# Layer 1's column products as eight 64x64 products in four array tiles, fed from a second copy of the own rows

## The chip, the cores and the metric

The kernel runs on one core of a Trainium2 chip. The metric is device time in microseconds. Three timed runs of the kernel before gave 908.75, 901.74 and 906.34 us, median 906.34 us. The profiled execution is a run of its own: 909.48 us, of which 907.7 us lie between the first and the last instruction. TensorE's granted clock over that execution was 0.957 of full speed.

## The reference, cut to what matters

A graph attention layer with four heads, then a second attention layer with one head, a residual and two layer norms, over 8 batches of 2048 nodes with 64 channels:

```python
h = einsum('bnc,hdc->bhnd', x, Wh)                       # 4 heads
scores = where(mask, einsum('...nd,...md->...nm', h, h), NEG)
out_h = einsum('...nm,...md->...nd', softmax(scores), h) + bh
z = leaky_relu(cat, 0.2);  h2 = einsum('bnk,dk->bnd', z, Wo)
# the same attention on h2 (one head), leaky_relu, layernorm
out = layernorm(x + that)
```

The mask is the adjacency matrix with its diagonal set. The graph given is sparse away from its first nodes, and the fast path of the kernel uses that. Because scores of layer 1 are `x_n Wh^T Wh x_m`, the kernel forms the 64x64 matrix `Wh^T Wh` of each head once (called `gram`) and multiplies only the rows of the attending nodes with it.

## The kernel before, in words

**Tiling.** 56 hub nodes (`HUB`) are treated apart, against all nodes, in a first stage. The other 1992 nodes form 166 sets of 12 (`SET`). For each set, the neighbours of its nodes are found from the adjacency matrix as a list of at most 128 nodes. Two sets make a group `g` (83 groups, `NG`). A tile holds two batches on its 128 partitions, 64 channels each (called the two halves below), and four such pairs `q` side by side.

**Layer 1's loop** is one Python loop over `i` from -4 to NG+2; one pass is called a step here. Its order is written out by hand, so each engine runs its instructions in the order in which the step emits them. Each step works on several groups at different depths. TensorE's order within a step is:

- L836 `scores`: 64x64 products of the gathered, turned rows `xTg` with the columns `y`.
- L532 `project`: 64x64 products of 96 columns with `whT`, in four array tiles (row half `s` by column half `j`).
- L861 `values`: 128x64 products of the weights `e` with gathered rows `g`.
- L895 `second_maps` (128x64), L905 `second_rows` (a 96-wide transpose), then L821 `columns`, then L513 `turn` (four 128x128 transposes of gathered rows), L878 `turn_values` (transposes of `osb`), L513 again, and the next step's L836.

**Columns.** `own_rows` (L815, on POOL, each second step) copies the rows of four sets out of `xT` into the tile `xo`, 128 partitions by 192 columns. `columns(g)` multiplies `xo` with `gram` for two heads: two products of 128x128 by 192 columns. `gram` is a 128x128 matrix for each head with the 64x64 matrix on both diagonal blocks and zeros elsewhere, so both halves are done at once. The result is copied by ACT (L827 `keep_columns`) into `y`, which `scores` uses later. The POOL copy emitted in step `i` serves the products of steps `i+2` and `i+3`.

**The other engines in a step.** POOL: two indirect gathers (L807, five groups ahead), each second step L815, in the first nine steps an adjacency piece (L689, and L696 after each second piece), from step 30 on each second step `add_beta` (L943), then L901, which copies the tile `own` out. DVE: L841 (mask the scores), L868 and L869 (divide the values, writing `osb`), L524, L900 (writes `own`; the tile has two buffers, so it waits for POOL's L901 of two steps before), L909 (writes `rowt`), and jobs of the neighbour search. ACT: L519, L1146 (two copies that free the banks of L513), L848, L827, L885.

**SP's queue** issues the transfers, in the order of the program: adjacency pieces (L684, one in each of steps 0 to 8, 480 KB each, read by POOL's L689 of the same step into one of three buffers), `table2`'s rows (L912, two in each step, waiting for DVE's L909), and from step 30 on in each even step eight loads of x (L939 `load_own`, 24 KB each), which POOL's L943 reads in the odd step after; L944 stores L943's result.

A second stage (layer 2) follows from about 602 us, which the change doesn't touch.

Of the kernel before, what the change touches and what calls it, by code (L numbers as in the profile page):

```python
# [30 lines left out]
F32 = mybir.dt.float32  # L31
# [328 lines left out]
def fast_kernel(ctx: ExitStack, tc: tile.TileContext, x, adj, Wh, bh, Wo, bo, gamma, beta, out, flag):  # L360


    nc = tc.nc
    B, N, C = x.shape
    H, D, _ = Wh.shape
    P = 128
    NB = N // P
    Q = B // 2
    HP = H // 2
# [4 lines left out]
    NS = (N - HUB) // SET  # L374
    NG = NS // 2
    M = SET * H
    GM = 2 * Q * SET
# [13 lines left out]
    work = stage.enter_context(tc.tile_pool(name="work", bufs=2))  # L391
# [7 lines left out]
    def half(k):  # L399
        return slice(k * 64, (k + 1) * 64)  # L400
# [14 lines left out]
    share = [const.tile([P, n], F32, name=f"share{k}") for k, n in enumerate([HALFN, HALFN, HALFN, 512, 512, 2 * 456])]  # L415
    wnat = share[3][:, :H * C].rearrange("p (h c) -> p h c", h=H)
    whT = early.tile([P, H * D], F32, name="whT")
    gram = early.tile([P, H, P], F32, name="gram")
# [93 lines left out]
        for q in range(Q):  # L512
            nc.tensor.transpose(tp[:, q * P:(q + 1) * P], rows[:, q, 1:1 + P], ident)  # L513

    def leaky(cat, n, name):

        z = work.tile([P, HP, 2, n], F32, tag="z", name=name, bufs=3)
        for hp in range(HP):
            nc.scalar.activation(z[:, hp], cat[:, :, hp * n:(hp + 1) * n], AF.Identity, bias=bhp[:, hp:hp + 1], scale=1.0)  # L519
        return z  # L520

    def leak(z):
        f = z.rearrange("p q s n -> p (q s n)")
        nc.vector.scalar_tensor_tensor(f, f, SLOPE, f, OP.mult, OP.max)  # L524

    def project(ot, cat, n):

        for hp in range(HP):
            for s in range(2):
                for j in range(2):  # L530
                    h = 2 * hp + j
                    nc.tensor.matmul(cat[half(j), s, hp * n:(hp + 1) * n], whT[half(s), h * D:(h + 1) * D],  # L532
                                     ot[half(s), h, :], start=True, stop=True)
# [97 lines left out]
    def hub_later(t, new):  # L631

        n = 2 * HUB
        osb = hub_osb[t]

        def turn_back():
            pt = bank[0]
            for v in range(2):
                for k in range(2):
                    nc.tensor.transpose(pt[:, (2 * v + k) * P:(2 * v + k + 1) * P], osb[:, v, k, :], ident)  # L640
            ot = held["oth", t] = work.tile([P, H, n], F32, tag="ot", name=f"otbh{t}")
            nc.scalar.copy(ot.rearrange("c h (w n) -> c h w n", w=8),  # L642
                           pt.rearrange("c (w n) -> c w n", w=8)[:, :, :HV].rearrange("c w (n h) -> c h w n", h=H))

        def through_heads():
            cat = new(f"cath{t}", "C")
            project(held.pop(("oth", t)), cat, n)
            z = held["zh", t] = leaky(cat, n, f"zh{t}")
            leak(z)

        def to_table():
            z = held.pop(("zh", t))
            ph = new(f"hh{t}", "S")
            for p in range(2):
                for hp in range(HP):

                    v = z[:, hp, p, :].rearrange("d (v k m) -> d k v m", v=2, k=2)
                    nc.tensor.matmul(ph[half(p), 0, :n], woT[:, hp, :], v, start=(hp == 0), stop=(hp == HP - 1))
            nc.vector.tensor_copy(ownh[:, t, :], ph[:, 0, :n])
            nc.tensor.transpose(ph[:n, 1, :P], ownh[:, t, :], ident)  # L660
            r = rowts[t]
            nc.vector.tensor_tensor(r[:n, 1:1 + P], ph[:n, 1, :P], bob[:n].rearrange("n p d -> n (p d)"), OP.add)
            dst = table2[:HUB, :].rearrange("n (q c) -> q n c", q=Q)
            for k in range(2):
                nc.sync.dma_start(out=dst[2 * t + k], in_=r[k * HUB:(k + 1) * HUB])

        return [turn_back, through_heads, to_table]

    hub_osb = {}
# [130 lines left out]
    held = {}  # L800
# [9 lines left out]
    def own_rows(m):  # L810

        w = min(4, NS - 4 * m)
        t = held["x", m] = work.tile([P, 2 * GM], F32, tag="xo", name=f"xo{m}", bufs=2)
        src = xT[:, :, HUB:].rearrange("c q (k s) -> c s q k", s=NS)[:, 4 * m:4 * m + w]
        nc.gpsimd.tensor_copy(t[:, :w * 48].rearrange("c (s q k) -> c s q k", s=w, q=Q), src)  # L815

    def columns(g, cat):

        n = min(4, NS - 4 * (g // 2)) * 48
        for k in range(2):  # L820
            nc.tensor.matmul(cat[:, k, 2 * GM:2 * GM + n], gram[:, g % 2 * 2 + k, :], held["x", g // 2][:, :n], start=True, stop=True)  # L821

    def keep_columns(g, cat):
        n = min(4, NS - 4 * (g // 2)) * 48
        if g % 2 == 0:
            held["y", g // 2] = work.tile([P, 2 * GM, H], F32, tag="yg", name=f"y{g // 2}", bufs=2)
        nc.scalar.copy(held["y", g // 2][:, :n, g % 2 * 2:g % 2 * 2 + 2], cat[:, :, 2 * GM:2 * GM + n].rearrange("p a n -> p n a"))  # L827

    def scores(g, sp):
        xt = held.pop(("T", 1, g)).rearrange("c j (q n) -> c j q n", q=Q)  # L830
# [184 lines left out]
    for g in range(LOOK - 2):  # L1015
        for j in range(2):
            gather(table1, 2 * g + j, 1, rows_tile)
    own_rows(0)
    own_rows(1)
    for t in range(2):  # L1020
        hub_end(t)
# [9 lines left out]
    def one(name, tag):  # L1031
        return psum1.tile([P, 2, 512], F32, tag=tag, name=name)
# [94 lines left out]
    for i in range(-4, NG + 3):  # L1127
# [6 lines left out]
        cat = one(f"cat{i}", "C") if i <= NG else None  # L1134
        if i < NG:
            ph, pr = cat[:, 0, 384:384 + GM], cat[:GM, 1, 384:512]
        else:
            cat = one(f"cat{i}", "S" if i == NG + 1 else "C")
            ph, pr = cat[:, 0, :GM], cat[:GM, 1, :P]
        if 0 <= i - 1 < NG:  # L1140
            project(held.pop(("ot", i - 1)), cat, GM)
            held["z", i - 1] = leaky(cat, GM, f"z{i - 1}")
        if 0 <= i + 2 < NG:
            t = held["T", 1, i + 2] = work.tile([P, 2, 512], F32, tag="xTg", name=f"xTg{i + 2}", bufs=3)
# [11 lines left out]
        if NG - LOOK <= i < NG - 1:  # L1156
            for j in range(2):
                k = 2 * (i - NG + LOOK) + j
                hub_block(k, rows_tile(f"gh{k}"))
        if i + 6 < NG and i % 2 == 0 and i >= -2:  # L1160
            own_rows((i + 6) // 2)
# [25 lines left out]
        if 0 <= i + 4 < NG + NG % 2:  # L1187
            columns(i + 4, cat)
# [7 lines left out]
        if 0 <= i + 4 < NG + NG % 2:  # L1196
            keep_columns(i + 4, cat)
# [226 lines left out]
    k = 9  # L1424
    for u in range(-3, NU + 5):
        if 0 <= u < NU:
            a = u % 2
# [10 lines left out]
        if 0 <= u + 1 < NU:  # L1438
            a = (u + 1) % 2
# [31 lines left out]
def gat_kernel(tc: tile.TileContext, x, adj, Wh, bh, Wo, bo, gamma, beta, out):  # L1471
    nc = tc.nc
    with tc.tile_pool(name="flags", bufs=1, space=bass.MemoryType.DRAM) as pool:
        flag = pool.tile([1, 1], I32, name="flag")
        with tc.manual_schedule():
            fast_kernel(tc, x, adj, Wh, bh, Wo, bo, gamma, beta, out, flag)
        again = nc.values_load(flag, min_val=0, max_val=1)
        with tc.If(again > 0):
            general_kernel(tc, x, adj, Wh, bh, Wo, bo, gamma, beta, out)
# [28 lines left out]
```

## Time and profile before

| what | value |
|---|---|
| three timed runs | 901.74 to 908.75 us, median 906.34 |
| profiled execution, span | 909.48 us, 907.7 us |
| first stage and start of layer 1's loop | 0 to 155.5 us |
| layer 1's steps 0 to 29 | 155.5 to 325.2 us |
| steps 30 to 73 | 325.2 to 553.1 us |
| steps 74 to the end of the loop | 553.1 to about 602 us |
| TensorE's products for the columns (L821) | 320 matmul records of 326 ns each in the loop |
| adjacency pieces (L684) after 155 us | 7 of 34, 170.6 to 206.8 us |
| loads of x (L939) | 168, 324.7 to 536.3 us |

How to read it: a page gives sums over the whole execution; the timeline gives single instructions, with the start, the duration, the engine, the program line, the operation, the tiles (written <- read), the count when several are merged, and in brackets how long the engine had been idle and what ended that. SPq and POOLq are the engines' own instruction queues, where transfers are issued. Products in fp32 show as two records each.

### The profile page before, as it was taken

The numbers are of one execution on the slowest core, as the hardware profiler recorded it, in microseconds if no ns is written. First come the engines' busy times: TensorE is split into PE (matmuls) and PEld (weight loads), VectorE is DVE, ScalarE is ACT, GpSimd is POOL, SyncE is SP. The second block draws the span as 40 slices with busy tenths as digits, with TensorE's granted clock in tenths as the row PEclk, the third lists the DMA queues.
The fourth block names the chain that finished last, engine by engine and source line by source line (L and its number), as shares of the span: only waits on it lengthen the run. The fifth ranks groups of instructions, "written<-read, shape, count | busy, mean of one in ns | idle before, by whom it ended". The sixth has DMA issues, their size and how long they took to land.

```text
span 907.7 us, 42895 instructions
## 1 busy us (share of the span) xinstructions
PE 777.0 (86%) x18437; PEld 660.8 (73%) x18437; DVE 613.0 (68%) x1376; ACT 524.7 (58%) x1128; POOL 540.8 (60%) x780
## 2 busy tenths in 40 slices
PE   4777778899999999999999999989988887878750
PEld 3555456678889998989998988878867776666540
DVE  3247974678988788775566566543677877777594
ACT  1333443555666767667676666735667766667541
POOL 4553241556455456656666665128888888888810
PEclk9899988999999999999999999999999999999975
DMA  8885540354333344444544443339756565555521
GB/s 182 234 238 174 138 117 24 111 134 118 88 82 94 86 117 134 129 125 135 132 125 121 125 125 99 104 111 287 197 151 170 167 166 165 145 151 153 149 68 28
DMA packets 81792, 122.54 MB, mean 135 GB/s; under 512 B 35568, under 2 KB 51852, under 8 KB 81594
## 3 DMA queue, kind: packets, MB, share of 16 engines
q0 software_dynamic: 26784, 65.84, 27.8%
q1 hardware_dynamic: 37702, 49.57, 18.2%
q10 hardware_dynamic: 17108, 4.30, 2.5%
q8 instruction: 148, 2.42, 1.1%
q14 instruction: 50, 0.41, 0.2%
HBM read 123.91 MB, written 18.48 MB: 157 GB/s over the span
## 4 chain that ended last, share of the span: by engine, by line
PE 51%; DVE 16%; POOL 11%; DMA 9%; issue 6%; ACT 4%; SPq 1%; POOLq 0%; ACTq 0%; DVEq 0%
PE o L861 9%; PE s L836 8%; POOL rows L807 8%; PE bank L513 7%; PE cat L821 5%; DMA raw<-in_adj_dram 5%; PE cat L532 3%; PE o L878 3%; DMA rows<-table,index 3%; PE t L513 3%; PE cat L895 3%; PE o L1279 2%; POOL space L1235 2%; PE cat L905 2%; DVE share L746 1%
## 5 line engine op out<-in xcount | busy, mean ns | idle before, releaser
L807 POOL DMA_INDIRECT g<-table,index x166 | 176.4, 1063 | 171.7 <-PE o L861 137.1
L807 POOL DMA_INDIRECT rows<-table,index x166 | 174.8, 1053 | 35.3 <-issue 18.3
L841 DVE TENSOR_TENSOR e<-s,mask 128x768 f32<-128x768 f32 x83 | 79.3, 955 | 79.4 <-PE s L836 75.7
L513 PE MATMUL t<-ident,rows 128*128 128x128 f32 x664 | 97.6, 283 | 35.7 <-DMA rows<-table,index 22.4
L513 PEld LDWEIGHTS t<-ident,rows 128*128 128x128 f32 x664 | 73.8, 143 | 52.7 <-issue 20.6
L519 ACT ACTIVATE z<-cat,bhp 128x192 f32<-128x192 f32 x166 | 60.7, 417 | 78.8 <-PE cat L532 78.7
L1398 ACT COPY xts<-t 128x512 f32<-128x512 f32 x166 | 90.6, 586 | 25.0 <-PE t L513 24.7
L513 PE MATMUL bank<-ident,g 128*128 128x128 f32 x664 | 100.7, 275 | 0.2 <-ACT otbh L642 0.2
L861 PE MATMUL o<-g,e 128*64 128x65 f32 x2656 | 96.5, 225 | 0.6 <-issue 0.6
L836 PE MATMUL s<-y,xTg 64*64 64x48 f32 x5312 | 95.4, 220 | 0.7 <-DVE share L717 0.7
L836 PEld LDWEIGHTS s<-y,xTg 64*64 64x64 f32 x5312 | 85.2, 134 | 14.6 <-issue 14.6
L861 PEld LDWEIGHTS o<-g,e 128*64 128x64 f32 x2656 | 84.7, 137 | 10.6 <-issue 0.7
L1146 ACT COPY xTg<-bank 128x512 f32<-128x512 f32 x166 | 89.1, 596 | 0.8 <-PE bank L513 0.8
L513 PEld LDWEIGHTS bank<-ident,g 128*128 128x128 f32 x664 | 80.3, 142 | 3.0 <-DVE keysi L774 0.6
L848 ACT ACTIVATE e<-e,shifts 128x768 f32<-128x768 f32 x83 | 80.0, 964 | 2.4 <-DVE e L841 2.0
L606 ACT ACTIVATE e<-e,shifts 128x896 f32<-128x896 f32 x32 | 33.3, 1043 | 79.5 <-DVE e L603 46.9
L689 POOL TENSOR_SCALAR a<-raw 120x1024 bf16<-120x1024 int32 (+1 forms) x34 | 38.2, 1128 | 67.7 <-DMA raw<-in_adj_dram 61.7
L827 ACT COPY y<-cat 128x384 f32<-128x384 f32 (+1 forms) x80 | 40.7, 509 | 65.3 <-DVE rowt L909 31.5
L821 PE MATMUL cat<-xo,gram 128*128 128x192 f32 (+1 forms) x320 | 65.0, 326 | 0.0
L868 DVE RECIPROCAL rall<-o 64x8 f32<-64x8 f32 x166 | 34.0, 205 | 43.6 <-PE o L861 42.0
L1279 PE MATMUL o<-rows,share 128*32 128x65 f32 x2656 | 52.7, 234 | 8.6 <-DVE share L1268 8.6
L869 DVE TENSOR_TENSOR osb<-o,rall 128x512 f32<-128x512 f32 x83 | 57.4, 691 | 2.9
(191 smaller groups left out, 1575.4 us busy)
## 6 DMA issues: line engine op xcount, KB each, us to landing
raw<-in_adj_dram SPq DMA_DIRECT2D x32, 480.0 KB
table<-xb SPq DMA_DIRECT2D x22, 256.0 KB
xr_s<-table SPq DMA_DIRECT2D x21, 256.0 KB
table<-x SPq DMA_DIRECT2D x16, 260.0 KB
x<-in_x_dram ACTq DMA_DIRECT2D x32, 128.0 KB
table<-rowt SPq DMA_DIRECT2D x164, 24.4 KB
xb<-in_x_dram SPq DMA_DIRECT2D x164, 24.0 KB
out_dram<-y_s SPq DMA_DIRECT2D x162, 24.0 KB
```

The costliest lines, as they stand in the source:

```text
L513: nc.tensor.transpose(tp[:, q * P:(q + 1) * P], rows[:, q, 1:1 + P], ident)
L519: nc.scalar.activation(z[:, hp], cat[:, :, hp * n:(hp + 1) * n], AF.Identity, bias=bhp[:, hp:hp + 1], scale=1.0)
L807: nc.gpsimd.indirect_dma_start(out=t.rearrange("n q c -> n (q c)"), out_offset=None, in_=table, in_offset=bass.IndirectOffsetOnAxis(ap=ind ...
L821: nc.tensor.matmul(cat[:, k, 2 * GM:2 * GM + n], gram[:, g % 2 * 2 + k, :], held["x", g // 2][:, :n], start=True, stop=True)
L836: nc.tensor.matmul(sp[half(r), p, (q * 2 + j) * M:(q * 2 + j + 1) * M], xt[half(p), j, q, half(r)], y[half(p), (j * Q + q) * M:(j * Q + q ...
L841: nc.vector.tensor_tensor(e[:, :16 * M].rearrange("p (a q n) -> p a q n", a=2, q=Q), sp[:, :, :8 * M].rearrange("p a (q n) -> p a q n", q= ...
L848: nc.scalar.activation(e[:, :16 * M], e[:, :16 * M], AF.Exp, bias=shifts[:, 0:1], scale=1.0)
L861: nc.tensor.matmul(op[half(p), j, o0:o0 + K1], e[:, c0:c0 + 64], rw[j][:, q, sums(p)], start=True, stop=True)
L869: nc.vector.tensor_tensor(osb, v[:, :, :, 1:K1], r.unsqueeze(3).to_broadcast([P, 4, 2, D]), OP.mult)
L1146: nc.scalar.copy(t[:, k, :], bank[k])
L1279: nc.tensor.matmul(op[t * 32:(t + 1) * 32, f, k * W2 + p:k * W2 + p + K1], e[:, 2 * q + p, k, :], rw[:, q, sums(p)], start=(a == 0 and k = ...
L1398: nc.scalar.copy(xts[s // 2 % 4][:, s % 2, :], tp)
```

## The change

`own_rows` issues, after POOL's copy, two transfers on SP's queue that copy each half of `xo`, the part that the other half of the array needs, into a new tile `xs` (128 partitions by 96 columns, two buffers). `columns` then makes each head's product as four 64x64 products of 96 columns: row half `r` of the array with the block of `gram` there, column half `p` of the array for the output. Where `r` equals `p` the moving operand is `xo`, else `xs`. So all four 64x64 tiles of the array take part, and each has half the columns. The copy out of PSUM (`keep_columns`) reads the new layout. To make room, the two hub tiles `zh` move from the ring of `z` into a tile that is free then (`share[5]`), which makes the ring's slots smaller.

```diff
-    def leaky(cat, n, name):
+    def leaky(cat, n, name, z=None):
-        z = work.tile([P, HP, 2, n], F32, tag="z", name=name, bufs=3)
+        if z is None:
+            z = work.tile([P, HP, 2, n], F32, tag="z", name=name, bufs=3)
...
-            z = held["zh", t] = leaky(cat, n, f"zh{t}")
+            z = share[5][:, t * 4 * n:(t + 1) * 4 * n].rearrange("p (a b n) -> p a b n", a=HP, b=2)
+            held["zh", t] = leaky(cat, n, f"zh{t}", z)
...
         nc.gpsimd.tensor_copy(t[:, :w * 48].rearrange("c (s q k) -> c s q k", s=w, q=Q), src)
+        other = held["xs", m] = work.tile([P, GM], F32, tag="xs", name=f"xs{m}", bufs=2)
+        n = w * 24
+        for p in range(2):
+            nc.sync.dma_start(out=other[half(p), :n], in_=t[half(1 - p), p * n:(p + 1) * n])
...
-        n = min(4, NS - 4 * (g // 2)) * 48
+        n = min(4, NS - 4 * (g // 2)) * 24
+        t, other = held["x", g // 2], held["xs", g // 2]
         for k in range(2):
-            nc.tensor.matmul(cat[:, k, 2 * GM:2 * GM + n], gram[:, g % 2 * 2 + k, :], held["x", g // 2][:, :n], start=True, stop=True)
+            h = g % 2 * 2 + k
+            for p in range(2):
+                for r in range(2):
+                    src = t[half(p), r * n:(r + 1) * n] if r == p else other[half(r), :n]
+                    nc.tensor.matmul(cat[half(p), r, 2 * GM + k * n:2 * GM + (k + 1) * n], gram[half(r), h, half(r)], src,
+                                     start=True, stop=True)
...
-        nc.scalar.copy(held["y", g // 2][:, :n, g % 2 * 2:g % 2 * 2 + 2], cat[:, :, 2 * GM:2 * GM + n].rearrange("p a n -> p n a"))
+        nc.scalar.copy(held["y", g // 2][:, :n, g % 2 * 2:g % 2 * 2 + 2].rearrange("p (r n) k -> p r n k", r=2),
+                       cat[:, :, 2 * GM:2 * GM + n].rearrange("p r (k n) -> p r n k", k=2))
```

Lines below the first edit move down: L684 becomes L686, L912 L925, L939 L952, L944 L957, L943 L956, L815 L817, L901 L914, L900 L913; the new transfers stand at L821 and the new products at L832.

The first place is SP's queue in steps 2 to 5 of the loop (`raw` is an adjacency piece, `rowt` a row that goes to the second table). Before:

```order
L684 DMA raw_0_1_1892<-in_adj_dram 120x1x1024
L684 DMA raw_1_0_2017<-in_adj_dram 120x1x1024
L665 DMA table_99<-rowt_112 56x130 x2
L684 DMA raw_1_1_2140<-in_adj_dram 120x1x1024
L684 DMA raw_2_0_2272<-in_adj_dram 120x1x1024
L912 DMA table_99<-rowt_112 4x12x130 x2
L665 DMA table_99<-rowt_113 56x130 x2
L684 DMA raw_2_1_2400<-in_adj_dram 120x1x1024
```

and now:

```order
L821 DMA xs_1919<-xo_1917 64x96 x2
L686 DMA raw_0_1_1928<-in_adj_dram 120x1x1024
L686 DMA raw_1_0_2058<-in_adj_dram 120x1x1024
L667 DMA table_99<-rowt_112 56x130 x2
L821 DMA xs_2180<-xo_2178 64x96 x2
L686 DMA raw_1_1_2190<-in_adj_dram 120x1x1024
L686 DMA raw_2_0_2327<-in_adj_dram 120x1x1024
L925 DMA table_99<-rowt_112 4x12x130 x2
L667 DMA table_99<-rowt_113 56x130 x2
L821 DMA xs_2460<-xo_2458 64x96 x2
L686 DMA raw_2_1_2464<-in_adj_dram 120x1x1024
```

In each even step the two copies into `xs`, the first of which waits for POOL's copy into `xo`, now stand ahead of the adjacency piece of that step.

The second place is the same queue from step 30 on (`xb` is the tile that the eight loads of x fill). Before:

```order
L939 DMA xb_148<-in_x_dram 12x2x256 x8
L912 DMA table_99<-rowt_115 4x12x130 x2
L944 DMA table_150<-xb_148 128x512
L912 DMA table_99<-rowt_112 4x12x130 x2
L939 DMA xb_149<-in_x_dram 12x2x256 x8
```

and now:

```order
L821 DMA xs_5688<-xo_5686 64x96 x2
L952 DMA xb_148<-in_x_dram 12x2x256 x8
L925 DMA table_99<-rowt_115 4x12x130 x2
L957 DMA table_150<-xb_148 128x512
L925 DMA table_99<-rowt_112 4x12x130 x2
L821 DMA xs_5941<-xo_5939 64x96 x2
L952 DMA xb_149<-in_x_dram 12x2x256 x8
```

The eight loads of an even step stood right behind the odd step's row transfers; now the two copies into `xs`, with their wait for POOL, stand between.

The third place is TensorE's queue in one step, from `second_rows` to the next `scores`. Before:

```order
L905 MATMUL cat_3433<-ident,own_3372 96x128
L821 MATMUL cat_3433<-xo_3118,gram 128x192 x2
L513 MATMUL bank_1710<-ident,g_32_3241 128x128 x4
L878 MATMUL o_3449<-ident,osb_3466 128x112 x4
L513 MATMUL bank_1711<-ident,g_33_3245 128x128 x4
L836 MATMUL s_3512<-y_3153,xTg_3445 64x48 x32
```

and now:

```order
L918 MATMUL cat_3179<-ident,own_3119 96x128
L832 MATMUL cat_3179<-xo_2970,gram 64x96
L832 MATMUL cat_3179<-xs_2972,gram 64x96 x2
L832 MATMUL cat_3179<-xo_2970,gram 64x96 x2
L832 MATMUL cat_3179<-xs_2972,gram 64x96 x2
L832 MATMUL cat_3179<-xo_2970,gram 64x96
L513 MATMUL bank_1716<-ident,g_26_2962 128x128 x4
L891 MATMUL o_3195<-ident,osb_3212 128x112 x4
```

Two products on the whole array, between transposes that also use it whole, have become eight on its quarters.

## The prediction

> **What bounds the kernel now.** I read the page first, then one step of layer 1's loop in the timeline, then the timeline of POOL and SP alone, because the change gives those two queues work. The page's busy times and its chain:
>
> ```profile
> PE 777.0 (86%) x18437; PEld 660.8 (73%) x18437; DVE 613.0 (68%) x1376; ACT 524.7 (58%) x1128; POOL 540.8 (60%) x780
> ...
> PE 51%; DVE 16%; POOL 11%; DMA 9%; issue 6%; ACT 4%; SPq 1%; POOLq 0%; ACTq 0%; DVEq 0%
> ```
>
> TensorE holds half of the chain, but that is a mean over stages. The changed work lies in layer 1's loop. One step of it in the timeline, with some rows of PEld (weight loads), DVE and ACT:
>
> ```profile
> 304.75 0.53 PE L532 MATMUL cat<-otb,whT 64*64 64x96 f32 x16
> ...
> 305.21 1.15 PE L861 MATMUL o<-g,e 128*64 128x65 f32 x32
> ...
> 306.62 0.31 PE L905 MATMUL cat<-ident,own 128*96 128x128 f32 x1
> ...
> 306.77 0.82 PE L821 MATMUL cat<-xo,gram 128*128 128x192 f32 x4
> 306.86 0.69 DVE L869 TENSOR_TENSOR osb<-o,rall 128x512 f32<-128x512 f32 x1
> ...
> 307.43 0.60 PE L513 MATMUL bank<-ident,g 128*128 128x128 f32 x4
> ...
> 307.75 0.45 PEld L878 LDWEIGHTS o<-ident,osb 112*128 112x128 f32 x4
> ...
> 307.86 0.55 PE L878 MATMUL o<-ident,osb 112*128 112x112 f32 x4
> ...
> 308.25 0.60 PE L513 MATMUL bank<-ident,g 128*128 128x128 f32 x4
> ...
> 308.78 1.15 PE L836 MATMUL s<-y,xTg 64*64 64x48 f32 x64
> ...
> 308.87 0.54 ACT L885 COPY otb<-o 128x192 f32<-128x192 f32 x2
> ...
> 309.75 0.53 PE L532 MATMUL cat<-otb,whT 64*64 64x96 f32 x16
> ```
>
> No PE row carries a bracket: TensorE waits for nothing, and from L532 to L532 a step takes 309.75 - 304.75 = 5.00 us. In such a step every tenth that TensorE saves is a tenth of time, until another engine's chain is in the way. Not all steps are like this:
>
> ```profile
> L861 PE MATMUL o<-g,e x2656: 218/222/271, 155.5 to 594.6; 128*64 128x65 f32 x190
> ```
>
> Between the starts of L861's 83 groups, 51 of the 82 distances in the timeline lie within 0.1 us of 5.00; the others are longer, with other engines ending them (a few at the end are shorter).
>
> **The products.** From L905 to L513 the step now takes 307.43 - 306.62 = 0.81 us. What replaces L821 has a twin: L532 is also eight 64x64 products of 96 columns in four tiles, and takes 305.21 - 304.75 = 0.46 us up to the next group's start, which has another array shape. Ahead of it stand L905's own 128 columns (four transposes of that size take 307.86 - 307.43 = 0.43 us, so 0.11) and the change of shape into 64x64: from the second L513 to L836 is 0.53 us for the same four transposes, so 0.10 more. Sum 0.11 + 0.10 + 0.46 = 0.67: **0.14 us less a step**. Bounds: 0.24 if the change of shape into the products were free, and a loss of 0.19 if only two tiles overlapped (the body 0.33 longer; the new loop has the row half innermost, L532 the column half). I take 0.14, since L532 is the same shape.
>
> The Trainium skill has a rule against this change: its page TensorEngine Tiling (Array Packing), Key Properties, says that a change of tiling mode drains TensorE. The 0.10 us above agrees with it, and by it the change adds two such drains a step; by its table of theoretical speedups alone an estimate would be nearer 0.33, half of L821's 0.66.
>
> Is there room for 0.14? `osb` is ready at 306.86 + 0.69 = 307.55 and L878's weights are loaded from 307.75: 0.20 of slack, enough. ACT's L885 ends at 309.41, 0.34 ahead of L532. The copy L827 keeps its 384 elements a partition; if its new pattern cost it 0.1, that slack would take it. Moving the hub tiles costs nothing: the same activations write them, and if their tile were not free they would wait in two steps alone.
>
> **The copies.** They move 84 x 24 KB, 2 MB beside 122.5 MB, so bandwidth is no term. The term is SP's queue: the first copy of an even step waits for POOL's L815, and what SP has to issue behind it waits as well. In steps 0 to 8 that is the adjacency piece which POOL's L689 reads in the same step; from step 30 on it is the eight loads that POOL's L943 reads in the next. In both places POOL then waits for a transfer that itself waited for POOL: a ring. Such a ring has a length of its own, whatever TensorE does.
>
> *The ring from step 30 on.* POOL and SP over two steps, the shortest loads on which POOL visibly waited, a pair of row transfers for the cost of issuing, and the columns that would use the copy:
>
> ```profile
> 449.91 1.04 POOL L807 DMA_INDIRECT g<-table,index  x1 [1.12 <-PE o L861]
> 450.30 3.47 SPq L939 DMA_DIRECT2D xb<-in_x_dram  x8
> 451.26 1.02 POOL L807 DMA_INDIRECT g<-table,index  x1 [0.30 <-PE cat L821]
> 452.28 0.53 POOL L815 COPY xo<-xT 128x192 f32<-128x192 f32 x1
> ...
> 457.66 1.27 POOL L943 TENSOR_TENSOR xb<-xb,bet 128x512 f32<-128x512 f32 x1 [0.38 <-DMA xb<-in_x_dram]
> 458.89 0.26 POOL L901 COPY own<-own 128x96 f32<-128x96 f32 x1
> ...
> 460.15 0.82 PE L821 MATMUL cat<-xo,gram 128*128 128x192 f32 x4
> ```
>
> ```profile
> 169.75 0.77 SPq L665 DMA_DIRECT2D table<-rowt  x2
> ...
> 347.89 4.11 SPq L939 DMA_DIRECT2D xb<-in_x_dram  x8
> ...
> 353.97 1.27 POOL L943 TENSOR_TENSOR xb<-xb,bet 128x512 f32<-128x512 f32 x1
> ```
>
> ```profile
> L943 POOL TENSOR_TENSOR xb<-xb,bet x22: 1267/1282/1292, 333.9 to 551.1; 128x512 f32<-128x512 f32 x22
> ```
>
> The ring in its order: an even step's gathers and L815, 449.91 to 452.81, 2.90; to SP and the two copies' issue, 0.05 + 0.77 (for 64 rows of 384 B the nearest is L665, 56 rows of 520 B, twice); from the first of the eight loads to L943, 353.97 - 347.89 = 6.08; L943 and L901, 459.15 - 457.66 = 1.49; to the next even gather about 0.15, as after other L901. Sum **11.4 us for two steps**. Before, the loads stand ahead of the gathers, and 21 distances of L943 take 551.1 - 333.9 = 217.2, or 10.34 each. So the ring falls behind by 1.1 a pair, 23 us in all. A lag of some 4 us costs nothing: the copy would land at about 452.81 + 0.05 + 0.77 + 2.3 = 455.9 (2.3 is from the start of the last of the eight issues, 0.4 before 352.00, to L943 at 353.97), and its products start at 460.15. That leaves **+19**. Bounds: with the other pass in which POOL waited, 457.66 - 450.30 = 7.36, the ring is 12.7 and the term 21 x 2.36 - 4 = +46; with 5.3, the landing of a bigger transfer below, it is 10.65 and the term +2.
>
> *The ring of steps 0 to 8.* POOL's busy time over those steps (the columns of the row are the stretch, its length, then PE, PEld, DVE, ACT and POOL), and single rows:
>
> ```profile
> 156.80:214.70 57.90, 51.12 (x1282) 44.39 (x1281) 41.98 (x111) 33.65 (x78) 36.88 (x49) 1.00 0.47 126
> ```
>
> ```profile
> 170.61 1.70 SPq L684 DMA_DIRECT2D raw<-in_adj_dram  x2
> ...
> 175.90 1.09 POOL L689 TENSOR_SCALAR a<-raw 120x1024 bf16<-120x1024 int32 x1 [1.84 <-DMA raw<-in_adj_dram]
> ...
> 186.91 1.52 SPq L684 DMA_DIRECT2D raw<-in_adj_dram  x1
> ...
> 193.92 1.14 POOL L689 TENSOR_SCALAR a<-raw 120x1024 bf16<-120x1024 int32 x1 [3.56 <-DMA raw<-in_adj_dram]
> ...
> 205.35 0.26 POOL L901 COPY own<-own 128x96 f32<-128x96 f32 x1
> ...
> 210.54 0.26 DVE L900 COPY own<-cat 128x96 f32<-128x96 f32 x1
> ...
> 214.36 0.26 POOL L901 COPY own<-own 128x96 f32<-128x96 f32 x1
> ...
> 223.88 0.27 POOL L901 COPY own<-own 128x96 f32<-128x96 f32 x1 [1.60 <-DVE own L900]
> ```
>
> A piece lands 175.90 - 170.61 = 5.3 to 193.92 - 186.91 = 7.0 us after its issue. Now POOL's 36.9 us have 21 of idle time between them, of which 5.4 is for pieces. With the change each of the five even steps waits 0.8 + 5.3 = 6.1 behind L815: 36.9 + 5 x 6.1 + 2.7 (nine gaps of 0.30 between gathers) = 70.1, so step 8's L901 ends near 227 instead of 214.6, 12 late, and step 6's 6 to 7 late. Who waits: DVE's L900 writes the tile that L901 of two steps before must have left. Step 8's L900 (210.54) has 210.54 - 205.61 = 4.9 of slack, step 10's (ending at 223.88) about 9. So TensorE, which waits for DVE through L909, L827 and L885, loses about 2 in step 8 and 2 in step 10: +4 with 5.3, by the same count +12 with 7.0. I take **+6**, nearer the pair that was issued without delay.
>
> *Sum.* The 0.14 is won only where no ring sets the pace: some 25 steps (12 to 30 and 76 on), -3.5. So -3.5 + 6 + 19 = +21.5. On the profiled execution's 909.5 that makes 931; the median of the runs shown is 3.1 lower, so **928 us**.
>
> **The rivals.** *Hidden copies.* They are issued two steps ahead of their use, SP is idle much of the time, and POOL in the page is only 60% busy; then the products' gain remains: 51 steps x 0.14 = 7, and about 1 from the start of the loop, so 898. For it speaks that the rings are about time to land, which the trace shows only with other neighbours; against it, that in two passes POOL already waits for these very loads with SP a whole row of transfers earlier. The Trainium skill's page DMA: Bandwidth & Descriptors, Rules for kernel authors, advises just this (issue early, wait late, and the fixed cost overlaps); it does not speak of what queues behind a transfer that has to wait for its source.
>
> *Only the early ring binds.* If the loads land in 5.3, the late term is +2 and the gain is won in most steps: -5.5 + 6 + 2 = +2.5, so 909.
>
> *Long landings.* With 7.36 the sum is -3.5 + 6 + 46 = +48.5, so 955.
>
> *Two tiles only.* If the four tiles don't overlap, the change doesn't do what it says: 0.19 longer in the 25 free steps, +5 instead of -3.5, so 936. L532's 0.46 speaks against it.
>
> **How the numbers follow.** Forecast (both rings bind) 0.60, own range 915 to 946; hidden copies 0.13; only the early ring 0.14; long landings 0.06; two tiles 0.07. The range that holds eight in ten is 898 to 948: below it lies half of the hidden case, above it the long landings and the forecast's tail. Faster by over 1% (below 897), which is about what a measurement of this kernel can tell from no change: 0.06. Within 1%: 0.07 from the hidden case, 0.11 from the early ring alone, 0.03 from the forecast's low end, 0.21. Slower by over 1%: 0.73.
>
> **What would show it.** Right: L943's instruction starts 11 to 12 us apart and its idle time is put down to the transfers into `xb`; L689 waits some 5 us in even steps 0 to 8; the products' line in even steps waits for the transfers into `xs`, and DVE's L900 for POOL's L901; in steps 12 to 30 the step is 4.86. Wrong: steps at 4.86 after step 40 (the late ring does not bind), or L905 to L513 at 0.81 or more (the products are no faster).

## The result and the profile after

The changed kernel takes **956.54 us** (median of 4 runs) where the kernel before takes 904.04 us (4 runs): 1.0568 times, 95% interval 1.0513 to 1.0624. On another chip the same pair measured 957.45 against 909.26, 1.0501 (1.0424 to 1.0577). (The ratios and intervals here and below are taken from undisturbed runs alone, and can differ by some thousandths from the quotient of the two medians.) So it is slower by some 50 us, in the forecast's direction and beyond its range of 898 to 948. The profiled execution took 956.55 us, span 954.8.

The page's busy times and its chain:

```profile
PE 796.3 (83%) x19445; PEld 655.6 (69%) x19445; DVE 613.6 (64%) x1376; ACT 525.6 (55%) x1128; POOL 538.9 (56%) x780
...
PE 37%; POOL 18%; DVE 15%; DMA 12%; issue 9%; ACT 4%; SPq 3%; POOLq 1%; ACTq 0%; DVEq 0%
```

TensorE has 1008 more product records, and its share of the chain falls from 51% to 37%; POOL goes from 11% to 18%, transfers from 9% to 12%, SP's queue from 1% to 3%. What grew is, for the most part, what passes through POOL and SP.

**Where the time is.** ACT's exponentials stand once in each of the 83 groups. Their row in the kernel before (count, duration, first and last start), and then after:

```profile
L848 ACT ACTIVATE e<-e,shifts x83: 935/965/968, 153.9 to 589.8; 128x768 f32<-128x768 f32 x83
```

```profile
L861 ACT ACTIVATE e<-e,shifts x83: 935/965/974, 148.9 to 638.8; 128x768 f32<-128x768 f32 x83
```

The loop takes 489.9 us instead of 435.9: **54.0 us more**, all of the loss. (The loop of the kernel before starts 5 us later in its profiled execution, since TensorE's granted clock fell to 0.52 to 0.83 in parts of 132 to 152 us there; in the traces of two kernels below it starts at 147 us.) Single starts of the same rows, read from the timelines:

```
group        0      13      33      40      50      60      70      82
before  153.90  232.41  336.89  372.50  424.86  475.28  528.34  589.81
after   148.93  235.44  341.79  383.90  444.44  506.68  565.87  638.78
shift    -4.97   +3.03   +4.91  +11.40  +19.58  +31.40  +37.52  +48.97
```

So the early steps lose 8.0, groups 13 to 33 lose 1.9, and the rest loses **44.1**.

**The late ring.** POOL over one turn, then SP's transfers in it:

```profile
442.18 1.27 POOL L956 TENSOR_TENSOR xb<-xb,bet 128x512 f32<-128x512 f32 x1 [4.29 <-DMA table<-rowt]
443.41 0.25 POOL L914 COPY own<-own 128x96 f32<-128x96 f32 x1
443.83 1.04 POOL L809 DMA_INDIRECT g<-table,index  x1 [0.17 <-PE o L874]
...
446.13 1.02 POOL L809 DMA_INDIRECT g<-table,index  x1 [1.25 <-PE o L891]
447.15 0.51 POOL L817 COPY xo<-xT 128x192 f32<-128x192 f32 x1
...
454.87 1.26 POOL L956 TENSOR_TENSOR xb<-xb,bet 128x512 f32<-128x512 f32 x1 [4.51 <-DMA table<-rowt]
```

```profile
447.69 1.18 SPq L821 DMA_DIRECT2D xs<-xo  x2
448.91 4.08 SPq L952 DMA_DIRECT2D xb<-in_x_dram  x8
```

The order is the one predicted: POOL's L956, its gathers and L817, 0.03 us later the two transfers, then the eight loads, and POOL stands idle until they have landed. The row of L956 gives the length of a turn:

```profile
L956 POOL TENSOR_TENSOR xb<-xb,bet x22: 1263/1270/2221, 342.3 to 598.4; 128x512 f32<-128x512 f32 x22
```

(598.4 - 342.3) / 21 = **12.2 us** for two steps, where it was 10.34. TensorE now waits for the copies, and DVE for TensorE (the waits between 30 and 620 us: total, times, longest):

```profile
POOL xb L956 <- DMA table<-rowt: 69.5, 15, 5.8
...
POOL xb L956 <- DMA xb<-in_x_dram: 32.9, 7, 6.4
...
PEld cat L832 <- DMA xs<-xo: 20.2, 12, 2.9
DVE own L913 <- PE cat L832: 18.3, 14, 3.4
PE cat L832 <- DMA xs<-xo: 17.9, 11, 2.7
```

L956 reads only `xb`; its 15 waits put to `table` are the same wait, named after another transfer that ended late in that queue: the loads' issue in the turn above ends 448.91 + 4.08 = 452.99, and L956 starts 1.9 later.

The granted clock is not what lengthens the turns: over them (342 to 599 us) it was 0.95 here, and 0.99 over those of the kernel with the transfers alone (345 to 602 us, below), which are as long.

**The early ring**, waits between 155 and 216 us, in the kernel before and then after:

```profile
POOL a L689 <- DMA raw<-in_adj_dram: 5.4, 2, 3.6
```

```profile
POOL a L691 <- DMA raw<-in_adj_dram: 26.5, 4, 6.9
...
DVE own L913 <- POOL own L914: 6.5, 2, 6.1
```

POOL waits 26.5 us for the pieces instead of 5.4.

**A step without waits**, TensorE:

```profile
279.87 0.31 PE L918 MATMUL cat<-ident,own 128*96 128x128 f32 x1
280.11 0.29 PE L832 MATMUL cat<-xo,gram 64*64 64x96 f32 x1
...
280.63 0.66 PE L513 MATMUL bank<-ident,g 128*128 128x128 f32 x4
281.12 0.55 PE L891 MATMUL o<-ident,osb 112*128 112x112 f32 x4
...
283.01 0.53 PE L533 MATMUL cat<-otb,whT 64*64 64x96 f32 x16
283.47 1.15 PE L874 MATMUL o<-g,e 128*64 128x65 f32 x30
```

From L918 to L513 it takes 0.76 us here (0.736 in the median of such steps; 0.803 before), and from L513 to the next group 0.49 instead of 0.43. Such a step takes 4.985 instead of 4.997 us (medians): the products win 0.012 us a step, not 0.14.

### The profile page after: what moved, and what is told of

Read it like the earlier page. It is cut to its first block, busy times and chain, and to the rows that moved or that the text cites. A ratio compares the mean times of both kernels' runs of the same rounds, so it can differ in the third digit from the quotient of the medians.

```text
span 954.8 us, 45049 instructions
## 1 busy us (share of the span) xinstructions
PE 796.3 (83%) x19445; PEld 655.6 (69%) x19445; DVE 613.6 (64%) x1376; ACT 525.6 (55%) x1128; POOL 538.9 (56%) x780
## 3 DMA queue, kind: packets, MB, share of 16 engines
q8 instruction: 155, 2.54, 1.1%
## 4 chain that ended last, share of the span: by engine, by line
PE 37%; POOL 18%; DVE 15%; DMA 12%; issue 9%; ACT 4%; SPq 3%; POOLq 1%; ACTq 0%; DVEq 0%
POOL rows L809 9%; PE o L874 6%; PE bank L513 6%; PE s L849 6%; DMA raw<-in_adj_dram 4%; DMA xs<-xo 3%; PE cat L832 3%; POOL g L809 3%; POOL space L1248 3%; PE cat L533 3%; PE o L891 2%; DMA rows<-table,index 2%; PE t L513 2%; SPq L952 2%; PE cat L908 2%
## 5 line engine op out<-in xcount | busy, mean ns | idle before, releaser
L809 POOL DMA_INDIRECT g<-table,index x166 | 171.6, 1034 | 98.8 <-PE o L874 58.9
L513 PE MATMUL t<-ident,rows 128*128 128x128 f32 x664 | 99.0, 283 | 38.4 <-DMA rows<-table,index 26.0
L513 PEld LDWEIGHTS t<-ident,rows 128*128 128x128 f32 x664 | 73.5, 143 | 57.3 <-ACT xts L1411 27.8
L513 PE MATMUL bank<-ident,g 128*128 128x128 f32 x664 | 111.2, 293 | 0.9 <-ACT otbh L643 0.4
L874 PE MATMUL o<-g,e 128*64 128x65 f32 x2656 | 100.3, 228 | 4.5 <-issue 4.4
L849 PE MATMUL s<-y,xTg 64*64 64x48 f32 x5312 | 98.5, 223 | 1.1 <-DVE share L719 0.7
L849 PEld LDWEIGHTS s<-y,xTg 64*64 64x64 f32 x5312 | 87.8, 137 | 16.2 <-issue 16.0
L874 PEld LDWEIGHTS o<-g,e 128*64 128x64 f32 x2656 | 87.6, 141 | 15.4 <-issue 5.7
L691 POOL TENSOR_SCALAR a<-raw 120x1024 bf16<-120x1024 int32 (+1 forms) x34 | 38.2, 1127 | 94.3 <-DMA raw<-in_adj_dram 86.9
L956 POOL TENSOR_TENSOR xb<-xb,bet 128x512 f32<-128x512 f32 x22 | 28.9, 1312 | 102.4 <-DMA table<-rowt 69.5
L513 PEld LDWEIGHTS bank<-ident,g 128*128 128x128 f32 x664 | 78.0, 148 | 11.7 <-issue 1.8
L832 PE MATMUL cat<-xs,gram 64*64 64x96 f32 (+1 forms) x640 | 45.7, 262 | 17.9 <-DMA xs<-xo 17.9
```

Of the source, the lines that this page charges most:

```text
L809: nc.gpsimd.indirect_dma_start(out=t.rearrange("n q c -> n (q c)"), out_offset=None, in_=table, in_offset=bass.IndirectOffsetOnAxis(ap=ind ...
L832: nc.tensor.matmul(cat[half(p), r, 2 * GM + k * n:2 * GM + (k + 1) * n], gram[half(r), h, half(r)], src, start=True, stop=True)
L849: nc.tensor.matmul(sp[half(r), p, (q * 2 + j) * M:(q * 2 + j + 1) * M], xt[half(p), j, q, half(r)], y[half(p), (j * Q + q) * M:(j * Q + q ...
L874: nc.tensor.matmul(op[half(p), j, o0:o0 + K1], e[:, c0:c0 + 64], rw[j][:, q, sums(p)], start=True, stop=True)
```

## The experiments

Each edit is against the changed kernel unless something else is said. The theory at the start: the loss is two rings through SP's queue. The rivals: the products that now wait for a transfer; the traffic; the changes of array shape.

**The transfers without the products.**

```diff
     def columns(g, cat):
...
-                    src = t[half(p), r * n:(r + 1) * n] if r == p else other[half(r), :n]
-                    nc.tensor.matmul(cat[half(p), r, 2 * GM + k * n:2 * GM + (k + 1) * n], gram[half(r), h, half(r)], src,
-                                     start=True, stop=True)
+            nc.tensor.matmul(cat[:, k, 2 * GM:2 * GM + n], gram[:, g % 2 * 2 + k, :], held["x", g // 2][:, :n], start=True, stop=True)
...
```

> The two transfers into xs stay where the change puts them, but nothing reads them: the products are the old 128x128 ones on xo. Queue theory (SP holds what is behind a transfer that waits for POOL, and POOL then waits for that): the two rings need nobody who reads xs, so most of the loss stays, 940 to 956 us, with add_beta's distances still near 12.3 us and POOL's wait for the adjacency pieces as in the changed kernel. Rival, waiting products (TensorE stands idle because its products now need a transfer: the changed kernel's trace puts 38 us of TensorE's idle time, weights and products together, to xs): without a reader the loss goes, 900 to 912. Rival, shape changes (the 64x64 products with their changes of array shape are what costs): also 900 to 912.

950.58 us against 906.13: 1.0465 (1.0405 to 1.0525). Nothing reads `xs`, and nearly nine tenths of the loss stays (44 of 50 us). Its `add_beta` (L956 in the changed kernel) is L949:

```profile
L949 POOL TENSOR_TENSOR xb<-xb,bet x22: 1259/1267/1551, 345.1 to 601.9; 128x512 f32<-128x512 f32 x22
```

(601.9 - 345.1) / 21 = 12.2 us. The ring needs nobody who reads `xs`; the 18 to 20 us for which TensorE (products, weight loads) waits on `xs` in the changed kernel are a place where the delay shows, not its cause.

**The loads ahead of the transfers.**

```diff
+        if i % 2 == 0 and 0 <= (i - 30) // 2 <= NV:
+            load_own((i - 30) // 2)
         if i + 6 < NG and i % 2 == 0 and i >= -2:
             own_rows((i + 6) // 2)
...
-        if 0 <= (i - 30) // 2 <= NV:
-            (add_beta if i % 2 else load_own)((i - 30) // 2)
+        if i % 2 and 0 <= (i - 30) // 2 <= NV:
+            add_beta((i - 30) // 2)
```

> The changed kernel, but in the even steps from 30 on the eight loads into xb are issued ahead of own_rows, so only the transfers stand behind POOL. Queue theory: the late ring (44 us between step 33 and the loop's end in the traces) is gone and the early one (some 8) stays: 908 to 916, add_beta's distances back at 10.0 to 10.4 us. Rival, waiting products: the transfers now go out some 3.5 us later in the queue, behind eight issues, so the products wait longer: 960 to 985.

919.6 us, 1.0127 (1.0069 to 1.0186). The same instructions, one place changed on SP:

```profile
L956 POOL TENSOR_TENSOR xb<-xb,bet x22: 1276/1282/1298, 345.3 to 568.4; 128x512 f32<-128x512 f32 x22
```

10.62 us a turn. Some 37 us come back, although the transfers now stand behind eight issues. The time is still some 4 us above what was expected. Against the kernel before, the exponentials shift by 9.1 us between the groups 0 and 13 in this trace: the early ring is as it was.

**The transfers last in the step**, and the same with the tiles in another order.

```diff
             keep_rows(i - 3, pr)
+        if i + 6 < NG and i % 2 == 0 and i >= -2:
+            send_rows((i + 6) // 2)
```

(`send_rows` holds the two transfers, which `own_rows` no longer issues.)

> The changed kernel with the same transfers, issued as the last thing of the even step on SP's queue, behind the adjacency piece, the eight loads and the two rows of keep_rows. Queue theory: both rings are gone, and the step is the 4.985 us of the undisturbed steps: 900 to 907, that is, the same as the kernel before within 0.5%, since a product step of 4.985 against 4.997 is worth 1 us. If the products were worth the 0.14 us a step of the prediction: 893 to 897. Rival, waiting products: the transfers land still later, so 955 or more. Rival, traffic (13440 more packets on the queues slow the others): 930 to 950 wherever they are issued.

914.45 us, 1.0090 (1.0052 to 1.0128). Both rings are gone: the row of `add_beta` gives (558.8 - 333.9) / 21 = 10.7 us a turn, and the exponentials shift by less than 1 us between the groups 0 and 13. But 8 us are left, outside what any theory had said (the trace counts 6720 more packets than the kernel before, not 13440). The interval overlaps that of the loads first, so the early ring's share is known from the traces only.

> As the kernel with the transfers last, and the eight products of a step issued with the column half innermost, as in L533, which takes 0.456 us up to the next group where the products take 0.492. If the order of the tiles is what makes the 0.036 us: products at 0.456 and 83 x 0.036 = 3 us less than the kernel with the transfers last. If the 0.036 and the 0.055 of the next group are the change of array shape back to 128x128: the same time within 1 us, products still at 0.49.

917.64 us, 1.0102 (1.0064 to 1.0141), the products at 0.492 us in both traces. The order of the tiles changes nothing in them.

**Four kernels on a slower chip.** This set ran on a chip on which the kernel before takes 1020.87 us; only ratios and traces within it are compared.

> The kernel with the transfers last, but with the old 128x128 products; nothing reads xs. It tells what the remaining 8 us (914.45 against 906.13) of the kernel with the transfers last hang on. Theory of the longer program (1008 more products and as many weight loads on TensorE, and stalls of TensorE that wait for nothing the profile shows, 8.8 us of them of over 0.4 us in that trace against 1.9 before): without the products the 8 us go, 903 to 909. Rival, traffic of the transfers (6720 more packets): they stay, 911 to 917.

1023.6 us, 1.0036 (1.0002 to 1.0070): with the old products, the transfers at the end of the step cost some 3 us of 1021 on this chip, at the edge of what the interval can tell from nothing.

> The changed kernel with one of its two transfers where it is, and the other at the end of the step. A test of the late ring's sum: the two issues measure 1.22 to 1.9 us there, one would take 0.6, so each pair of steps gets 0.6 to 0.7 shorter (12.32 to 11.65 in add_beta's distances): 21 x 0.65 = 14 us less, and some 2 less in the early ring, so 938 to 944. If it were the wait of the products for both transfers, and not the length of what POOL waits for: 955 or more, since the second one now lands later.

1083.12 us, 1.0623 (1.0578 to 1.0668).

> The changed kernel with the transfers of the steps up to 20 at the end of their step, and the later ones where the change puts them. The early ring alone is undone: from the traces (8.3 us from step 0 to step 14) 946 to 951. If the two rings were one loss that only shifts (the late ring taking up what the early one had delayed), it would be 954 to 958, as the changed kernel.

1085.27 us, 1.0631 (1.0598 to 1.0665). With the changed kernel not among them, the two times can't be set against it, and the absolute numbers expected miss by the chip. Between the two the ring can be read, with one transfer and then with both ahead of the loads:

```profile
L960 POOL TENSOR_TENSOR xb<-xb,bet x22: 1262/1270/1282, 369.6 to 635.2; 128x512 f32<-128x512 f32 x22
```

```profile
L959 POOL TENSOR_TENSOR xb<-xb,bet x22: 1262/1272/1883, 366.5 to 641.3; 128x512 f32<-128x512 f32 x22
```

12.65 and 13.09 us a turn: a transfer less ahead of the loads shortens it by 0.44, where 0.65 was expected. Issue time counts in the ring. What the early ring alone costs in time stays open.

> The kernel with the transfers last, with the eight products moved between the scores and L533, which have the same 64x64 shape, and the second transposition of gathered rows ahead of turn_values, so that osb still has its time. Theory of shape changes: L918's 0.244, the products' 0.492 and L513's 0.492 go back to 0.11 + 0.437, and the products cost the 0.44 of their twin: 4.985 - 0.68 + 0.44 = 4.74 to 4.80 a step, 12 to 18 us less than with the transfers last, if the chains of VectorE and ScalarE leave room: 896 to 904. If the products cost the same wherever they stand: 4.98 and the same time as with the transfers last. If the longer program's stalls take what a shorter step gives: steps of 4.75 in the timeline, but 908 to 914.

1035.79 us, 1.0157 (1.0094 to 1.0220). In this trace TensorE's records pause in most steps inside the scores' run (L852), with nothing that they wait for (71 times, 30.2 us in all; 16 times and 4.1 us in the trace with the old products on the same chip), so that most steps are 5.4 to 5.9 us long. Why, the runs don't show.

**Four on one chip of the usual speed.**

> The changed kernel once more, as the measure for the three beside it on the same chip, since the kernels of the last set ran on a chip on which the kernel before takes 1020.87 us and where TensorE waits much longer for nothing that the profile shows. Both theories: 1.05 to 1.075 times the kernel before.

957.45 us, 1.0501 (1.0424 to 1.0577): the loss of the changed kernel again.

> The kernel with the transfers last, beside its twin with the old products on one chip. Theory of the longer program: this one is slower than its twin by what TensorE waits more in the rows put down to issue, 5 to 9 us on a chip as the first, 10 to 20 on one as the second. Rival, traffic: both the same within 2 us, and both slower than the kernel before by 5 to 10.

917.1 us, 1.0081 (1.0043 to 1.0119).

> The twin with the old products and the transfers last. Theory of the longer program: the same as the kernel before within 4 us. Rival, traffic: 5 to 10 us slower than the kernel before.

909.21 us, 0.9988 (0.9952 to 1.0024). So the transfers, issued last, cost nothing that these runs can tell, and traffic is out as the cause of the 8 us. The moved hub tiles are in this twin too, so they are out as well. **The new products cost 8 us net.** The exponentials' rows of the two, with the new products and with the old:

```profile
L864 ACT ACTIVATE e<-e,shifts x83: 935/965/970, 147.0 to 595.5; 128x768 f32<-128x768 f32 x83
```

```profile
L857 ACT ACTIVATE e<-e,shifts x83: 935/966/971, 146.9 to 586.5; 128x768 f32<-128x768 f32 x83
```

448.5 against 439.6 us, and TensorE's waits at the values (L877, L870) in each:

```profile
PEld o L877 <- issue: 10.2, 10, 2.5
PE o L877 <- issue: 8.8, 9, 2.4
PEld cat L835 <- DMA xs<-xo: 2.6, 2, 1.4
PE cat L835 <- DMA xs<-xo: 2.2, 2, 1.2
```

```profile
PEld o L870 <- issue: 3.5, 7, 1.0
...
PE o L870 <- issue: 2.5, 4, 0.9
```

The longest such stall, and the stretches around it (stretch, its length, then the engines' busy times, granted clock, DMA share, GB/s):

```profile
579.16 0.34 PE L877 MATMUL o<-g,e 128*64 128x65 f32 x4
581.88 1.78 PE L877 MATMUL o<-g,e 128*64 128x65 f32 x28 [2.39 <-issue]
```

```profile
582.00:584.00 2.00, 2.00 (x36) 2.00 (x36) 0.27 (x2) 0.00 (x0) 0.00 (x0) 0.50 0.04 8
584.00:586.00 2.00, 2.00 (x25) 1.46 (x24) 1.75 (x5) 0.03 (x1) 0.25 (x1) 0.50 0.30 34
586.00:590.00 4.00, 4.00 (x112) 3.55 (x112) 0.86 (x1) 1.37 (x5) 0.02 (x1) 0.75 0.37 124
```

TensorE stops in the middle of a run of equal products, with no tile to wait for. The granted clock behind the stop is 0.50 up to 588 us and 1.00 from there (the 0.75 of the last row is the mean of the two). Counted through TensorE's records of the trace, the record after each of these stops is number 193 or 194 modulo 256: ten gaps of over 0.25 us between weight loads in the loop with the new products, 10.2 us together, eight with the old ones, 5.0 us, all at the same two remainders. So the stops lie, to within one record, a multiple of 256 instructions apart: they are at ends of blocks of 256, though at most of the some 97 blocks of the loop TensorE doesn't stop. The page's row for the instruction queue, with the new products and then with the old:

```profile
q8 instruction: 155, 2.54, 1.1%
```

```profile
q8 instruction: 147, 2.41, 1.1%
```

Eight blocks of 16 KB more. So: 5.2 us of longer stops, 2.2 to 2.6 of waits for `xs`, some 3 for the slow clock after one stop (6 us at half), less 1 for the 0.012 a step, 9.5 in all, against the loop's 448.5 - 439.6 = 8.9. The sum leaves out 3.4 us at half clock in the loop with the old products (from 177.6 us), and single starts of the two rows show that the loss is not spread evenly:

```
group             0      40      70      80      81      82
old products  146.90  366.93  525.31  577.23  582.03  586.45
new products  147.03  367.95  527.68  580.86  591.05  595.47
shift          +0.13   +1.02   +2.37   +3.63   +9.02   +9.02
```

The one long stop and the slow clock behind it make 5.4 us of the 8.9, between the groups 80 and 81. In the two earlier traces with the new products and the transfers last, TensorE stops at the same instruction for 2.25 us. Without the 2016 instructions the blocks end elsewhere. So it is shown that the stops are at the ends of blocks, and that their number and length differ; why TensorE stops at these ends and not at others stays open, and that fewer instructions elsewhere would give the 5 us back was not tried.

> The kernel with the products beside L533, on the same chip as the others. Theory of shape changes and longer program together: its undisturbed step is 4.75 us; on a chip as the first, where the stalls are some 9 us in all, 5 to 15 us less than the kernel with the transfers last, so at or below the kernel before; on one as the second, the stalls set the step (5.5 us there) and it is no faster than the kernel with the transfers last.

924.2 us, 1.0138 (1.0070 to 1.0205): not the 5 to 15 us less that were expected. Whether it is slower than with the products in their place (1.0081), the intervals don't tell. Its undisturbed step:

```profile
288.00 0.26 PE L835 MATMUL cat<-xo,gram 64*64 64x96 f32 x1
...
288.35 0.54 PE L533 MATMUL cat<-otb,whT 64*64 64x96 f32 x16
288.82 1.15 PE L877 MATMUL o<-g,e 128*64 128x65 f32 x32
...
290.24 0.31 PE L921 MATMUL cat<-ident,own 128*96 128x128 f32 x1
290.39 1.04 PE L513 MATMUL bank<-ident,g 128*128 128x128 f32 x8
```

takes 4.76 us: the eight products 0.35, L921 to L513 0.15. So beside products of their own shape they cost less than the prediction gave them, and the place, with the second transposition ahead of `turn_values`, is worth 4.985 - 4.76 = 0.225 us a step; what got shorter is the products and the rows at the changes of shape. But the products now stand some 2 us earlier, and the transfers at the end of the step come too late: TensorE waits 17.2 us for `xs` (14 times), weight loads 19.9.

**Taking the gathers out of the ring.** Own rows ahead of the step's gathers; in the other two the products beside L533 as well.

```diff
+        if i + 6 < NG and i % 2 == 0 and i >= -2:
+            own_rows((i + 6) // 2)
         if 0 <= i + LOOK < NG and i > -3:
             for j in range(2):
                 gather(table1, 2 * (i + LOOK) + j, 1, rows_tile)
...
-        if i + 6 < NG and i % 2 == 0 and i >= -2:
-            own_rows((i + 6) // 2)
```

> The changed kernel with own_rows (POOL's copy and, behind it on SP, the two transfers) ahead of the step's two gathers instead of behind them; nothing else. The ring's sum: POOL's copy no longer waits for the gathers, which wait for TensorE, so a turn is L956 and L914 1.49 + 0.2, POOL's copy 0.5, the two issues 1.3, the loads 6.2: 9.7 us for two steps, less than the 9.97 of two undisturbed steps. So the late ring no longer sets the pace; 8 us for the products' longer program and some for turns that come out longer: 917 to 930. If what counts is that SP waits for POOL at all, whatever POOL has to do before: 950 to 960, as the changed kernel.

927.24 us, 1.0146 (1.0083 to 1.0210), where the changed kernel has 1.0501 and 1.0568: some 30 us less by one copy's place among POOL's gathers, with SP still waiting for POOL. A turn:

```profile
L956 POOL TENSOR_TENSOR xb<-xb,bet x22: 1264/1272/1282, 337.7 to 574.6; 128x512 f32<-128x512 f32 x22
```

11.28, not 9.7. SP in one of them shows what the sum left out, the store of L956's result and two rows ahead of the transfers:

```profile
510.07 0.36 SPq L957 DMA_DIRECT2D table<-xb  x1
510.49 1.25 SPq L925 DMA_DIRECT2D table<-rowt  x2
511.78 1.40 SPq L821 DMA_DIRECT2D xs<-xo  x2
513.22 4.32 SPq L952 DMA_DIRECT2D xb<-in_x_dram  x8
```

L956 ends 510.04, so 1.74 us of SP's own work stand between it and the transfers.

> The changed kernel with own_rows ahead of the gathers, and the eight products between the scores and L533 (with the second transposition ahead of turn_values). Its undisturbed step measured 4.76. Two of them are 9.52, a turn of the ring by its sum 9.7: a small loss of some 4 us late in the loop; 83 x 0.226 = 19 us gained over the kernel with the transfers last (1.008 times before), minus these: 900 to 908, at or below the kernel before. If the stalls at the ends of blocks of TensorE's program grow as the steps get shorter: 908 to 915. If the ring is as long as it was: 950 or more.

927.43 us, 1.0196 (1.0152 to 1.0240). The steps are 4.73 to 4.79 us where nothing waits, but L956's distances are 11.3 us here too: a shorter step behind the same ring was worth nothing.

> As first_ahead, but the two transfers stand on SP behind the step's adjacency piece or eight loads, ahead of the two rows of keep_rows. No ring by construction; the transfers go out at most 3.5 us later, and their products stand at the beginning of the step after the next. If they land in time (4.2 us after the first issue, from 5.3 to 6 us of time): 897 to 904, the best of all; if not, TensorE waits 1 to 2 us in each even step from 30 on, as in the kernel with the products first and the transfers last (37 us of waits of PE and PEld together there): 905 to 920.

912.52 us, 1.0028 (0.9989 to 1.0067): the lowest ratio with the new products, and no different from the kernel before. It still waits for `xs` (8.6 us of TensorE) and for ACT's copy of the products (3.5). No version here was measured faster than the kernel before.

## Why the prediction was right or wrong

**Right in direction and mechanism.** Both rings are there, link by link: TensorE's line waits for `xs`, L691 for the pieces (up to 6.9 us), L913 for POOL's L914, L956 stands at 12.2 us, just outside the 11 to 12 given. That SP's place, and not the reading of `xs`, makes them was shown by the transfers alone (950.58) and by the loads first (919.6).

**The early ring, +6:** 8.0 in the changed kernel's trace, 9.1 in that of the loads first. Near, and inside its bounds of 4 to 12.

**The late ring, +19: this is the step that failed, by its size.** It was 44.1. The prediction's turn of 11.4, put together in four parts, and the same parts in the trace, the mean of the first 20 turns:

```
part                                      predicted  measured
L956 to the end of L817                        4.54      4.75
L817 to the first transfer                     0.05      0.03
issue of the two transfers                     0.77      1.33
first load's issue to the next L956            6.08      6.21
sum                                           11.44     12.32
```

Most of the difference is the issue: I priced a transfer of 64 rows from SBUF at that of L665's 56 rows, 0.385 each, and the two take 1.17 us or more in every turn. Over all 21 distances a turn is 12.20 by L956's row, 0.76 above my sum, and that makes 16 us: a ring that turns 21 times multiplies each tenth by 21. The other 9 us are lag, first of all the 4 us that I gave away free. Part of it was the landing, 3.1 us after the first issue by my sum; in the turn above the products start 451.86 - 447.69 = 4.2 us after it. The other part is that L956 lags by 8.4 us in its first turn already (342.3 against 333.9), while the steps are 4.9 behind: so 3.5 us of slack were used before the ring began to count. The rival "long landings" came to 955 and so near to the measured time, but that is luck: it had loads that land in 7.36, and they landed in 6.21 on average.

**The products, -3.5 in 25 free steps: this failed too, by its price.** The free step was to be 4.86 and is 4.985, so 25 of them win 0.3 us, and with all its waits the stretch of the groups 13 to 33 lost 1.9. The twin L532 has the same shape, yet it stands next to L836, of that shape as well. The products stand between two groups of 128x128 shape. L905 to L821 was 0.15; L918 to L832 is 0.244, so the way in costs 0.09, as predicted. The products up to L513 are 0.492, not 0.46, and the first L513 is 0.055 longer; I had no term for the way out. Moving them beside L533 gave 4.76. My own mark, L905 to L513 below 0.81, was met (0.736) and told nothing, since it ends ahead of the group that pays for the way out. The Trainium skill's page TensorEngine Tiling (Array Packing), Key Properties, says that a change of mode drains TensorE; weighed against the row it was the better guide, and the two changes that the new place saves (0.225 us a step) are together more than the gain that I had counted.

**What no step had:** 2016 more instructions for TensorE. The new products cost the kernel with the transfers last 8 us net against its twin (917.1 against 909.21), most of it by stops at ends of blocks of instructions and the slow clock behind one of them. In the prediction the count of instructions was no term at all. That it is the count that does it, and not where the blocks happen to end, no run shows.

## What to carry to other kernels

Before a transfer that waits for an engine is put on a shared queue, write down what stands behind it and who waits for that; if the list comes back to the same engine, add up the turn, and remember that each mispriced tenth counts once per turn. Issue such a transfer last: then it cost nothing here that could be measured, as long as its reader stood late enough (with the products earlier in the step it came too late). Products in another array shape belong next to products of that shape. Splitting products adds instructions; a step without waits doesn't show what these cost, so measure the whole loop.

## What the runs showed of the hardware

- TensorE stopped at some ends of blocks of 256 instructions, for 0.3 to 2.5 us, most often where the program runs fast (the values, 64 records in a microsecond). The Trainium skill's page Runtime: NRT & Kernel Launch, Instruction fetch mechanics, gives the block as 16 KiB, which the queue's rows agree with (2.54 MB in 155), and calls the crossing mostly hidden; in the loop with the transfers last it was 10.2 us in ten places.
- After a stop of 2.39 us, which ended at 581.88 us, the granted clock was 0.50 until 588 us and then 1.00 again.
- A 24 KB copy between the halves of SBUF takes SP some 0.6 us to issue. Where TensorE waited for two of them, it went on 4.2 us after the first issue in the turn shown, and 3.8 to 4.5 us after it in eleven of the twelve such waits of the changed kernel.
